# Convolutional attention block: how the first stage's normalisation steps are placed on the vector queue, where the first projections are accumulated, and which part of the values' tile is cleared

## Chip, core and metric

The kernel runs on one core of a Trainium2 chip as one launch. The metric is device time in microseconds (us), lower is better. The time before is the median of 3 runs.

## The reference, cut to what matters

The input is x, 8 images of 384 channels on a 32x32 grid, all float32. Four layers each add something to x. The change touches only the beginning of the first one:

```python
x = x + _L0(_gn(x), ...)          # _gn: 32 groups of 12 channels, mean and variance per image

def _dwproj(x, dw, g, b, pw):     # three times: for q, k and v
    y = conv3x3_depthwise(x, dw)
    y = gelu(_bn(y, g, b))        # _bn: mean and variance over all 8 images and the grid
    return einsum('oc,bchw->bohw', pw, y)

q, k, v = (_dwproj(x, ...).reshape(B, 8, 48, N) for each)
attn = softmax(einsum('bhcn,bhcm->bhnm', q, k) * scale)
out = _bn(einsum('oc,bchw->bohw', w_out, einsum('bhnm,bhcm->bhcn', attn, v)))
```

The batch norm over all images forces two passes. All depthwise convolutions have to be done, and their moments known, before the first gelu. The other layers (a mixture of experts, a ternary convolution, a deformable attention) are not touched.

## The kernel before

**First stage, about 0 to 230 us.** x is read from HBM as 16 tiles `xs`, normalised in place, convolved on TensorE, and written back raw to two scratch tensors in HBM, `rqk` and `rv`. The queues of all five engines are in an order written out by hand here (`manual_schedule`), so the order of the Python calls is the order of every queue.

The stage has eight *units* u = 0 to 7. A unit is two images (2k, 2k+1) and one half of the channels (h), that is two tiles xs (j = 0 and 1, one an image), each with two groups of rows (g). A unit's convolutions are cut into *pieces*, numbered n = 0 to 39 through the stage. Units 0 to 5 have five, `y0 a1 y1 a2 v0`; unit 6 has the first four; unit 7 has six, `y0 a1 y1 a2 v-1 v0`. "(u, i)" is piece i of unit u. A piece y is 48 matmul records, a piece a 96, a piece v 192 (L570[...]). For each piece, in this order on the queues:

1. some steps of the group normalisation of a later unit (below),
2. TensorE: the piece's matmuls into four banks of PSUM (`banks`), alternately four tiles of one bank each and two tiles `big` of two banks each. Two pieces can therefore be in PSUM at a time,
3. ScalarE: the copies of the four banks to a tile `y` in SBUF (L581, four copies of 512 columns or two of 1,024); `y` has four buffers,
4. VectorE: `bn_stats` of the four quarters of `y` (L587),
5. SyncE (SP): four DMAs of `y` to `rqk` or `rv` (L601). Up to two parts of a later tile xs (L292), or of image 0's raw maps (`g`, L225), are issued by SP ahead of the piece.

`norm(u)` makes the steps of a unit's normalisation. `begin(j)`: for both g, three `bn_stats` of xs (L351) and one `bn_aggr` (L354). `finish()`: a chain of small VectorE operations (L366 to L378), one power on GpSimd (L98), three more on VectorE (L380, L381, L385), of which the last writes `gss`, scale and shift. `apply(g, j)`: one ScalarE activation over 1,536 columns (L396) and two small products on GpSimd (L399). The table `steps` says which of a unit's seven steps is issued ahead of which piece:

```python
at = [(u - 2, 4) if u > 1 else (0, 0), (u - 1, 0), (u - 1, 0)]
at += [(u - 1, t) for t in range(1, 5)]
```

So `begin(0)` stands ahead of the last piece of unit u-2, `begin(1)` and the whole `finish` ahead of piece y0 of unit u-1, and the four `apply` ahead of that unit's next four pieces.

**End of the stage.** `spread_qk` and `spread_v` bring the moments of the maps together over partitions (matmuls `pmove` and `pmovev`) and `scale_of` makes scale and shift of the batch norm. `x_moments` has eight DMAs of SP (L508), ahead of the first piece of unit 7. `gelu_image` works on the raw maps of image 0. The first projections (L258) make q and k of the first pair of heads: for each of v = 0, 1 a tile `pq{v}_first` of two banks, of which `product` fills one half and then the other; each half is copied to `first_qk` (L620).

**Start of the attention stage, from 240 us.** `values_tile` makes the two tiles `vt` (128 partitions x 4,096), which hold the values as the second matmul of the attention wants them: blocks of 32 columns, of which 24 (`HQ0`) are values (L713, from `pv`), one is 1.0 (L688), and the rest zero. Each tile is cleared whole on GpSimd (L681) before. GpSimd is given the two clearings and then the two fills of ones. The attention's matmuls are `s` (L815) and `pav` (L830); `p` is the exponential on ScalarE (L822). From here on a scheduler orders all queues but ScalarE's.

Of the kernel before, what the change touches and what calls it, by code (L numbers as in the profile page):

```python
# [14 lines left out]
P = 128  # L15
KC = C // P
HALF = N // 2
# [12 lines left out]
HQ0 = HD0 // 2  # L30
# [25 lines left out]
def tile_kernel(ctx: ExitStack, tc: tile.TileContext, i: dict, out: bass.AP):  # L56
# [210 lines left out]
    with ExitStack() as pa:  # L267
# [71 lines left out]
        def norm(u):  # L339

            k, h = divmod(u, 2)
            mv = mvs[u % 2]
            turned = sa.tile([P, 2, 32], F32, tag="gp_t", name=f"gt{u}")
            rows = sa.tile([P, 2, 2, 16], F32, tag="gp_r", name=f"gr{u}")
            ss = sa.tile([P, 2, 32], F32, tag="gp_ss", name=f"gss{u}")
            small_ = sa.tile([P, 40], F32, tag="gp_s", name=f"gs{u}")

            def begin(j):
                for g in range(2):
                    for c in range(KC):  # L350
                        nc.vector.bn_stats(  # L351
                            xst[:, 2 * h + g, 2 * k + j, c, :], xs_of[2 * u + j][:, g * KC + c, :]
                        )
                    nc.vector.bn_aggr(  # L354
                        mv[:, :, 2 * j + g],
                        xst[:, 2 * h + g, 2 * k + j].rearrange("p c s -> p (c s)"),
                    )

            def finish():

                def owned(t):
                    return t.rearrange("p (g m d) -> p g m d", g=2, d=4)[:, :, :, 1:3]

                m8, v8, rs = small_[:, 0:2], small_[:, 2:4], small_[:, 4:6]
                dm, var, wide = small_[:, 8:40], turned[:, 1, :], [P, 2, 16]
                nc.vector.transpose(  # L366
                    turned.rearrange("p t y -> p (t y)"), mv.rearrange("p t y -> p (t y)")
                )
                nc.vector.tensor_reduce(m8, owned(turned[:, 0, :]), AX.XY, ALU.add)
                nc.vector.scalar_tensor_tensor(  # L370
                    dm.rearrange("p (g y) -> p g y", g=2), m8.unsqueeze(2).to_broadcast(wide),
                    -0.125, turned[:, 0, :].rearrange("p (g y) -> p g y", g=2),
                    ALU.mult, ALU.add,
                )
                nc.vector.tensor_tensor(dm, dm, dm, ALU.mult)
                nc.vector.tensor_tensor(dm, dm, var, ALU.add)
                nc.vector.tensor_reduce(v8, owned(dm), AX.XY, ALU.add)
                nc.vector.tensor_scalar(v8, v8, 0.125, 1e-5, ALU.mult, ALU.add)  # L378
                rsqrt(rs, v8, 2)
                nc.vector.tensor_copy(rows[:, 0], rs.unsqueeze(2).to_broadcast(wide))  # L380
                nc.vector.scalar_tensor_tensor(  # L381
                    rows[:, 1], m8.unsqueeze(2).to_broadcast(wide), -0.125, rows[:, 0],
                    ALU.mult, ALU.mult,
                )
                nc.vector.transpose(  # L385
                    ss.rearrange("p t y -> p (t y)"), rows.rearrange("p t g y -> p (t g y)")
                )

            def apply(g, j):
                n = 2 * j + g  # L390
                d = xs_of[2 * u + j][:, g * KC : g * KC + KC, :]
                sc, sh = ss[:, 0, n : n + 1], ss[:, 1, n : n + 1]
                if u == 0 and j == 1:
                    nc.vector.tensor_scalar(d, d, sc, sh, ALU.mult, ALU.add)
                else:
                    nc.scalar.activation(d, d, AF.Identity, bias=sh, scale=sc)  # L396
                for e, row in enumerate((0, HALF - W)):
                    f = d[:, :, row : row + W]
                    nc.gpsimd.tensor_tensor(  # L399
                        f, f, mrow[:, e : e + 1].unsqueeze(2).to_broadcast([P, KC, W]),  # L400
                        ALU.mult,
                    )

            return [lambda: begin(0), lambda: begin(1), finish] + [
                lambda g=g, j=j: apply(g, j) for g in range(2) for j in range(2)
            ]

        NU0 = 2 * NK
        work = []
# [3 lines left out]
        first = [[w[0] for w in work].index(u) for u in range(NU0)]  # L413
        steps = {}
        for u in range(1, NU0):
            at = [(u - 2, 4) if u > 1 else (0, 0), (u - 1, 0), (u - 1, 0)]
            at += [(u - 1, t) for t in range(1, 5)] if u < NU0 - 1 else [
                (u - 1, 1), (u - 1, 2), (u - 1, 3), (u, 0)
            ]
            for t, key in enumerate(at):  # L420
                steps.setdefault(key, []).append((u, t))

        def spread_qk():

            zs, nv, ng = (zy, zqk.rearrange("p c g s -> p (c g) s")), (3, 2), 16
            at = [slice(0, 96), slice(96, 160)]
            both = [
                room[:, 0, d].rearrange("p (v s g) -> p v s g", v=n, s=2)
                for d, n in zip(at, nv)
            ]  # L430
            v0 = 0
            for z, n, dst in zip(zs, nv, both):
                masked(z, n, v0, dst)
                v0 += n
            yield
            pm = bank("pmove")
            for t, d in enumerate(at):
                nc.tensor.matmul(
                    pm[:, d], lhsT=sels[:, t, :], rhs=room[:, 0, d], start=True, stop=True,
                )  # L440
            got = room[:, 1, :96].rearrange("p (x g) -> p x g", g=16)
            nc.vector.tensor_tensor(
                got, pm[:, :96].rearrange("p (x g) -> p x g", g=16),
                msk[:, :16].unsqueeze(1).to_broadcast([P, 6, 16]), ALU.mult,
            )
            fy = fs[:, :6].rearrange("p (v s) -> p v s", v=3)
            nc.vector.reduce_sum(fy.rearrange("p v s -> p (v s)"), got, AX.X)
            got = room[:, 1, 96:].rearrange("p (x g) -> p x g", g=8)
            nc.vector.tensor_tensor(
                got, pm[:, 96:160].rearrange("p (x g) -> p x g", g=8),  # L450
                msk[:, 16:24].unsqueeze(1).to_broadcast([P, 8, 8]), ALU.mult,
            )
            f = fs[:, 8:16]
            nc.vector.reduce_sum(f, got, AX.X)
            nc.vector.tensor_copy(
                fqk[:, :, :, 1:], f.rearrange("p (v s c) -> p v s c", v=2, s=2)
            )
            nc.vector.tensor_copy(fqk[:, :, :, 0], fy[:, :2])
            nc.vector.tensor_copy(fv[:, :, 0], fy[:, 2])
            for v in range(2):  # L460
                scale_of(v, fqk[:, v])
# [13 lines left out]
        def spread_v():  # L475

            both = sa.tile([P, 32], F32, tag="bothv", name="bothv")
            masked(zv, 2, 5, both.rearrange("p (c s g) -> p c s g", c=2, s=2))
            yield
            pm = bank("pmovev")  # L480
            nc.tensor.matmul(pm[:, :32], lhsT=sels[:, 1, :], rhs=both, start=True, stop=True)
            got = sa.tile([P, 4, 8], F32, tag="gotv", name="gotv")
            nc.vector.tensor_tensor(
                got, pm[:, :32].rearrange("p (x g) -> p x g", g=8),
                msk[:, 16:24].unsqueeze(1).to_broadcast([P, 4, 8]), ALU.mult,
            )
            f = sa.tile([P, 4], F32, tag="gotf", name="gotf")
            nc.vector.reduce_sum(f, got, AX.X)
            nc.vector.tensor_copy(
                fv[:, :, 1:].rearrange("p s c -> p c s"), f.rearrange("p (c s) -> p c s", s=2)  # L490
            )
# [26 lines left out]
        for n, (u, kind, s) in enumerate(work):  # L518
# [20 lines left out]
            if n == len(work) - 2:  # L539
                spread = spread_qk()  # L540
                next(spread)
            if n % 2:
                banks = [bank(f"pk{n}_{r}") for r in range(4)]
                outs = [(t, r, 1) for r, t in enumerate(banks)]
            else:
# [68 lines left out]
        next(ends)  # L614
        first_qk = image("first_qk")
        for v in range(2):
            pq = big(f"pq{v}_first")
            for h in range(2):
                product(pq[:, h * HALF : (h + 1) * HALF], 0, 0, v, h)
                (nc.vector.tensor_copy if v else nc.scalar.copy)(  # L620
                    first_qk[:, v, h * HALF : (h + 1) * HALF], pq[:, h * HALF : (h + 1) * HALF]
                )
            if v == 0:
                for _ in ends:
                    pass
                scales = scale_of(2, fv)
# [41 lines left out]
    with ExitStack() as pb:  # L668
# [9 lines left out]

        def values_tile(s):
            t = wb.tile([P, NT8, 2 * NH0, 32], F32, name=f"vt{s}")  # L680
            zero = nc.gpsimd.memset(t, 0.0)  # L681

            tc.add_manual_dep(
                zero.ins, scales.ins.name, mybir.DependencyInfo(
                    mybir.DependencyClass.Sync, mybir.DependencyReason.DATA
                ), reason="scales first",
            )
            nc.gpsimd.memset(t[:, :, :, HQ0 : HQ0 + 1], 1.0)  # L688
            vts.append(t)

        values_tile(0)
# [1476 lines left out]
```

## Time and profile before

| | us |
|---|---|
| time before, median of 3 (lowest, highest) | 3506.04 (3503.85, 3506.84) |
| the profiled execution's own time | 3505.04 |
| its span from the first to the last instruction | 3503.2 |
| TensorE busy over the span | 3380.1 (96%) |
| VectorE, ScalarE, GpSimd busy | 1697.7, 1297.4, 211.0 |
| pieces of the first stage: first matmul to the last copy to `y` | 24.56 to 230.90 |
| first matmul `pav` of the attention | 255.36 |

The profile is one execution on the chip. In the timeline a row begins with start and duration in us, then engine, line, operation, what is written and read, and how many instructions are merged in the row. In square brackets stands the idle time of the engine just before, and what ended it. PE is TensorE, DVE VectorE, ACT ScalarE, POOL GpSimd, SP SyncE; SPq is its queue, which issues DMAs. A table by windows gives each engine's busy time in each stretch, the granted share of TensorE's full clock (PEclk), the mean busy share of the 16 DMA engines, and what they moved.

### The profile page before, as it was taken

To read this page: it belongs to the slowest core of one execution; us is meant where nothing else is said; L and a number is where in the kernel's file an instruction comes from. 1 tells how busy PE (TensorE), PEld (TensorE's weight loads), DVE (VectorE), ACT (ScalarE), POOL (GpSimd) and SP (SyncE) were. 2 spreads that over 40 slices of the span, in tenths; PEclk is the share of its full clock that TensorE was granted. 3 is DMA by queue.
4 is the path that set the end of the run, shared out by engine and by line. 5 is a ranking of instruction groups with operands and counts; after the bars stand their busy time and mean duration, and the time that the engine had idled before them with its cause. 6 is when DMAs were issued, how large, how long until landed. Compare 5 with 4: busy or idle time off the path is not lost.

```text
span 3503.2 us, 44910 instructions
## 1 busy us (share of the span) xinstructions
PE 3380.1 (96%) x18599; PEld 1467.3 (42%) x18599; DVE 1697.7 (48%) x2881; ACT 1297.4 (37%) x1514; POOL 211.0 (6%) x231
## 2 busy tenths in 40 slices
PE   6889999999999999998999999999999999999888
PEld 3433434343434343443344445344453444534434
DVE  7862232323232323234266475663756637566573
ACT  4655444444444444433222322323223232232222
POOL 2110000000000000000000200102001020010112
PEclk9899999999999999999999999999999999999898
DMA  9972121212121212022600111101101011110000
GB/s 355 281 219 79 26 79 27 79 27 79 26 79 26 79 26 79 26 79 101 245 24 18 45 48 35 39 18 47 45 35 39 18 47 46 35 39 18 0 36 19
DMA packets 86259, 234.01 MB, mean 67 GB/s; under 512 B 21672, under 2 KB 21896, under 8 KB 79130
## 3 DMA queue, kind: packets, MB, share of 16 engines
q1 hardware_dynamic: 83882, 222.75, 19.9%
q10 hardware_dynamic: 1248, 4.72, 0.4%
q8 instruction: 150, 2.46, 0.3%
q0 software_dynamic: 912, 3.53, 0.3%
q14 instruction: 67, 0.55, 0.0%
HBM read 145.77 MB, written 75.59 MB: 63 GB/s over the span
## 4 chain that ended last, share of the span: by engine, by line
PE 42%; DVE 9%; ACT 1%; DMA 1%; issue 0%; POOL 0%; DVEq 0%; ACTq 0%; SPq 0%; POOLq 0%
PE y L1497 12%; PE ph L1476 9%; DVE y L1572 5%; PE pq L1617 4%; PE pw L1580 3%; PE pf L1924 3%; PE s L1795 2%; PE pav L1821 2%; DVE hd L1462 1%; PE pk L1770 1%; PE pv L1779 1%; PE pss L1834 1%; DMA o<-o 1%; PE xsb L1756 1%; PE plog L1226 1%; DVE off L1687 1%
## 5 line engine op out<-in xcount | busy, mean ns | idle before, releaser
L822 ACT ACTIVATE p<-s 128x1024 f32<-128x1024 f32 x512 | 496.3, 1021 | 368.7 <-PE s L815 368.5
L830 PE MATMUL pav<-p,vt 64*64 64x512 f32 x4096 | 494.7, 589 | 2.8 <-POOL vt L688 2.8
L1497 PE MATMUL y<-hd,w_sb 128*128 128x512 f32 x1080 | 488.7, 600 | 3.5 <-DVE hd L1462 3.5
L1476 PE MATMUL ph<-h,w_sb 128*128 128x512 f32 x1104 | 486.8, 595 | 3.1 <-ACT h L1425 3.0
L815 PE MATMUL s<-qk,qk 48*64 48x512 f32 x2944 | 355.1, 592 | 0.0
L1476 PEld LDWEIGHTS ph<-h,w_sb 128*128 128x128 f32 x1104 | 206.9, 190 | 264.4 <-issue 249.6
L1497 PEld LDWEIGHTS y<-hd,w_sb 128*128 128x128 f32 x1080 | 200.0, 191 | 248.2 <-issue 234.8
L830 PEld LDWEIGHTS pav<-p,vt 64*64 64x64 f32 x4096 | 168.0, 133 | 277.1 <-issue 273.2
L791 DVE COPY ta<-pav 128x512 f32<-128x512 f32 (+1 forms) x65 | 44.2, 682 | 475.5 <-PE pav L830 475.5
L1486 ACT ACTIVATE hd<-ph,b_sb 128x512 f32<-128x512 f32 x180 | 122.7, 682 | 312.7 <-PE ph L1476 312.7
L1572 DVE SCALAR_TENSOR_TENSOR y<-h,tap,y 128x961 f32<-128x961 f32 (+1 forms) x192 | 234.0, 1243 | 0.6
L570 PE MATMUL pk<-xs,cws_sb 32*32 32x496 f32 (+3 forms) x3840 | 175.4, 643 | 52.7 <-ACT y L581 26.0
L1687 DVE SCALAR_TENSOR_TENSOR off<-q,dw_sb,off 128x225 f32<-128x225 f32 (+3 forms) x432 | 212.0, 545 | 1.6
L815 PEld LDWEIGHTS s<-qk,qk 48*64 48x64 f32 x2944 | 109.3, 133 | 211.4 <-issue 190.5
L1812 ACT ACTIVATE p<-s 128x1024 f32<-128x1024 f32 x96 | 96.1, 1022 | 166.6 <-PE s L1795 141.7
L81 DVE COPY qk<-pq 128x512 f32<-128x512 f32 x46 | 31.8, 691 | 251.9 <-PE pq L258 251.9
L570 PEld LDWEIGHTS pk<-xs,cws_sb 32*32 32x32 f32 (+1 forms) x3840 | 87.2, 114 | 139.2 <-issue 53.5
L1462 DVE TENSOR_TENSOR hd<-hd,cb 128x512 f32<-128x512 f32 x180 | 122.4, 685 | 41.0 <-ACT hd L1486 40.8
L1580 PE MATMUL pw<-y,upw 128*128 128x512 f32 x288 | 130.4, 607 | 4.0 <-DVE y L1572 4.0
L1857 POOL TENSOR_TENSOR p<-p,p 128x1024 f32<-128x1024 f32 x48 | 112.9, 2354 | 349.9 <-ACT p L1812 349.8
L706 PE MATMUL pv<-wv_sb,g 128*128 128x384 f32 x384 | 127.2, 489 | 1.4 <-ACT g L243 1.4
L815 PE MATMUL s<-ql,ql 48*64 48x512 f32 x1024 | 128.2, 592 | 0.2 <-ACT p L822 0.2
(326 smaller groups left out, 3722.6 us busy)
## 6 DMA issues: line engine op xcount, KB each, us to landing
rqk<-y SPq DMA_DIRECT2D x96, 256.0 KB
g<-rqk SPq DMA_DIRECT2D x96, 256.0 KB
xs<-in_xs_dram SPq DMA_DIRECT2D x56, 384.0 KB
g<-rv SPq DMA_DIRECT2D x48, 256.0 KB
xh<-in_x_dram SPq DMA_DIRECT2D x48, 256.0 KB
f<-in_x_dram SPq DMA_DIRECT2D x24, 512.0 KB
f<-o SPq DMA_DIRECT2D x24, 512.0 KB
o<-ot SPq DMA_DIRECT2D x42, 256.0 KB
```

The costliest lines, as they stand in the source:

```text
L570: nc.tensor.matmul(banks[r][cols[q]].rearrange("p (h w) -> p h w", w=W)[:, :, c0:c1], lhsT=cws[rs, c, 2 * h + g, x, w], rhs=src[rs, :, c0 ...
L706: nc.tensor.matmul(pv[:, :C], lhsT=acts[b][2][:, c, t * P : (t + 1) * P], rhs=w_in[2][:, c, :], start=(c == 0), stop=(c == KC - 1),)
L815: nc.tensor.matmul(s[64 * k : 64 * k + 64, j * HALF : (j + 1) * HALF], lhsT=kt[r, k0 : k0 + 64], rhs=qt[r, h * HALF : (h + 1) * HALF], sta ...
L822: nc.scalar.activation(p, s, AF.Exp, scale=scale)
L830: nc.tensor.matmul(pav[k][64 * j : 64 * j + 64, :], lhsT=vts[b % 2][r, kc, 2 * hd : 2 * hd + 2, :].rearrange("p a b -> p (a b)"), rhs=p[r, ...
L1462: nc.vector.tensor_tensor(hd, hd, state["cb"], ALU.mult)
L1476: nc.tensor.matmul(ph, lhsT=w1[:, e, c, dc * P : (dc + 1) * P], rhs=state["h1"][c], start=(c == 0), stop=(c == KC - 1),)
L1497: nc.tensor.matmul(y, lhsT=w2[:, e, dc, m * P : (m + 1) * P], rhs=state[h, k], start=(k == 0), stop=(k == NE * KC - 1),)
L1572: nc.vector.scalar_tensor_tensor(d, f, tap2[:, c, t : t + 1], d, ALU.mult, ALU.add)
L1580: nc.tensor.matmul(pw[h], lhsT=upw2[:, c, m * P : (m + 1) * P], rhs=y[c][:, hs], start=(c == 0), stop=(c == KC - 1),)
L1617: nc.tensor.matmul(pq[h], lhsT=wq3[:, c, m * P : (m + 1) * P], rhs=h3[h][:, c, :], start=(c == 0), stop=(c == KC - 1),)
L1687: nc.vector.scalar_tensor_tensor(d, f, dw3[:, t : t + 1], d, ALU.mult, ALU.add)
```

## The change

The steps of `norm` become ten in place of seven: four `begin(j, g)` of one tile and one group each, `sums` (the former `finish` up to the power on GpSimd), `spread` (the three operations after it), and four `apply` in the same order as before. They are given places over two units, one ahead of most pieces:

| step of unit u | ahead of piece, before | ahead of piece, after |
|---|---|---|
| the four quarters of `begin` | (u-2,4) two, (u-1,0) two | (u-2,2), (u-2,3), (u-2,4), (u-1,0) |
| `sums` | (u-1,0) | (u-1,0) |
| `spread` | (u-1,0) | (u-1,1) |
| the four `apply` | (u-1,1) to (u-1,4) | (u-1,2), (u-1,3), (u-1,4), (u,0) |

For unit 1 what would come earlier than piece (0,0) is ahead of that piece; for unit 7 the last two `apply` are both ahead of (7,0), since unit 6 has no fifth piece.

Which pieces use the four single banks and which the two double ones is exchanged, and `pmove` and `pmovev` go to a double tile. Each of the four first projections gets a single bank of its own. Of `vt` only the columns 24 to 31 of each block are cleared, 1,024 elements in a partition in place of 4,096, and so the copies of the values (L713) no longer touch what GpSimd clears. No DMA is added, removed or moved: SP's queue has the same instructions in the same order. On GpSimd the order is the same too.

```diff
-            def begin(j):
-                for g in range(2):
-                    for c in range(KC):
-                        nc.vector.bn_stats(
-                            xst[:, 2 * h + g, 2 * k + j, c, :], xs_of[2 * u + j][:, g * KC + c, :]
-                        )
-                    nc.vector.bn_aggr(
...
-            def finish():
+            def begin(j, g):
+                for c in range(KC):
+                    nc.vector.bn_stats(
+                        xst[:, 2 * h + g, 2 * k + j, c, :], xs_of[2 * u + j][:, g * KC + c, :]
                     )
+                nc.vector.bn_aggr(
+                    mv[:, :, 2 * j + g],
+                    xst[:, 2 * h + g, 2 * k + j].rearrange("p c s -> p (c s)"),
+                )
...
+            def sums():
...
                 rsqrt(rs, v8, 2)
+
+            def spread():
+
                 nc.vector.tensor_copy(rows[:, 0], rs.unsqueeze(2).to_broadcast(wide))
...
-            return [lambda: begin(0), lambda: begin(1), finish] + [
-                lambda g=g, j=j: apply(g, j) for g in range(2) for j in range(2)
-            ]
+            pairs = [(a, b) for a in range(2) for b in range(2)]
+            return (
+                [lambda j=j, g=g: begin(j, g) for j, g in pairs] + [sums, spread]
+                + [lambda g=g, j=j: apply(g, j) for g, j in pairs]
+            )
...
-            at = [(u - 2, 4) if u > 1 else (0, 0), (u - 1, 0), (u - 1, 0)]
-            at += [(u - 1, t) for t in range(1, 5)] if u < NU0 - 1 else [
-                (u - 1, 1), (u - 1, 2), (u - 1, 3), (u, 0)
-            ]
-            for t, key in enumerate(at):
+            at = [(u - 2, 2), (u - 2, 3), (u - 2, 4), (u - 1, 0), (u - 1, 0), (u - 1, 1)]
+            at += [(u - 1, 2), (u - 1, 3), (u - 1, 4), (u, 0)]
+            for t, (u0, n) in enumerate(at):
+                key = (0, 0) if u0 < 0 else (7, 0) if (u0, n) == (6, 4) else (u0, n)
                 steps.setdefault(key, []).append((u, t))
...
-            pm = bank("pmove")
+            pm = big("pmove")
...
-            pm = bank("pmovev")
+            pm = big("pmovev")
...
-            if n % 2:
+            if n % 2 == 0:
                 banks = [bank(f"pk{n}_{r}") for r in range(4)]
...
         for v in range(2):
-            pq = big(f"pq{v}_first")
             for h in range(2):
-                product(pq[:, h * HALF : (h + 1) * HALF], 0, 0, v, h)
+                pq = bank(f"pq{v}_first{h}")
+                product(pq, 0, 0, v, h)
                 (nc.vector.tensor_copy if v else nc.scalar.copy)(
-                    first_qk[:, v, h * HALF : (h + 1) * HALF], pq[:, h * HALF : (h + 1) * HALF]
+                    first_qk[:, v, h * HALF : (h + 1) * HALF], pq
                 )
...
             t = wb.tile([P, NT8, 2 * NH0, 32], F32, name=f"vt{s}")
-            zero = nc.gpsimd.memset(t, 0.0)
+            tf = t.rearrange("p t h d -> p (t h) d")
+            zero = nc.gpsimd.memset(tf[:, :, HQ0:], 0.0)
...
-            nc.gpsimd.memset(t[:, :, :, HQ0 : HQ0 + 1], 1.0)
+            nc.gpsimd.memset(tf[:, :, HQ0 : HQ0 + 1], 1.0)
```

More of the change, by code (lines that the diff above doesn't have):

```diff
@@ L346, in norm @@
             small_ = sa.tile([P, 40], F32, tag="gp_s", name=f"gs{u}")
-            def begin(j):
-                for g in range(2):
-                    for c in range(KC):
-                        nc.vector.bn_stats(
-                            xst[:, 2 * h + g, 2 * k + j, c, :], xs_of[2 * u + j][:, g * KC + c, :]
-                        )
-                    nc.vector.bn_aggr(
-                        mv[:, :, 2 * j + g],
-                        xst[:, 2 * h + g, 2 * k + j].rearrange("p c s -> p (c s)"),
-                    )
-            def finish():
+            def begin(j, g):
+                for c in range(KC):
+                    nc.vector.bn_stats(
+                        xst[:, 2 * h + g, 2 * k + j, c, :], xs_of[2 * u + j][:, g * KC + c, :]
+                    )
+                nc.vector.bn_aggr(
+                    mv[:, :, 2 * j + g],
+                    xst[:, 2 * h + g, 2 * k + j].rearrange("p c s -> p (c s)"),
+                )
+            m8, v8, rs = small_[:, 0:2], small_[:, 2:4], small_[:, 4:6]
+            dm, var, wide = small_[:, 8:40], turned[:, 1, :], [P, 2, 16]
+            def sums():
                 def owned(t):
                     return t.rearrange("p (g m d) -> p g m d", g=2, d=4)[:, :, :, 1:3]
-                m8, v8, rs = small_[:, 0:2], small_[:, 2:4], small_[:, 4:6]
-                dm, var, wide = small_[:, 8:40], turned[:, 1, :], [P, 2, 16]
                 nc.vector.transpose(
```

## The prediction

> **What bounds the kernel now.** The page has TensorE busy for 96% of the span and idle visibly only in its first slices, so I read the first 256 us alone, first TensorE's timeline. Once a unit it stands still before a piece a2:
>
> ```profile
> 64.26 21.97 PE L570 MATMUL pk<-xs,cws_sb 32*32 32x512 f32 x480 [4.31 <-ACT y L581]
> 89.77 21.99 PE L570 MATMUL pk<-xs,cws_sb 32*32 32x512 f32 x480 [3.53 <-ACT y L581]
> 116.20 20.83 PE L570 MATMUL pk<-xs,cws_sb 32*32 32x512 f32 x480 [4.44 <-ACT y L581]
> ```
>
> All such gaps from 24.56 us to the end of the pieces sum to 28.1 us. Next, who holds ScalarE's copy back (timelines of VectorE and ScalarE, unit 2):
>
> ```profile
> 84.18 0.24 DVE L354 BATCH_NORM_AGGREGATE mvs<-xst 128x2 f32<-128x18 f32 x1
> ...
> 87.30 0.25 DVE L385 STREAM_TRANSPOSE gss<-gr 128x64 f32<-128x64 f32 x1
> 87.47 2.43 DVE L587 BATCH_NORM_STATS2 sy<-y 128x6 f32<-128x512 f32 x4
> 87.58 1.67 ACT L396 ACTIVATE xs<-xs,gss 128x1536 f32<-128x1536 f32 x1 [5.32 <-DVE gss L385]
> ```
>
> ScalarE waits 5.3 us for `gss`, and the copies of a1 are queued behind that `apply`; a2 needs their banks. Then the table by windows, whose last three columns are PEclk, DMA share, GB/s:
>
> ```profile
> 75.00:100.00 25.00, 21.41 (x471) 10.36 (x457) 21.80 (x47) 16.02 (x20) 2.95 (x8) 0.93 0.92 311
> 125.00:150.00 25.00, 20.58 (x454) 11.05 (x444) 20.93 (x46) 14.60 (x20) 3.29 (x9) 0.86 0.91 252
> ```
>
> VectorE (third figure) has 21 to 22 of 25 us, and the 16 DMA engines stand at 0.91 or more in every window from 25 to 200 us, whatever they move. So two others are close behind the wait. SP's timeline agrees:
>
> ```profile
> 85.45 2.14 SPq L292 DMA_DIRECT2D xs<-in_xs_dram  x2
> 87.69 0.99 SPq L601 DMA_DIRECT2D rqk<-y  x2
> ...
> 208.63 7.50 SPq L508 DMA_DIRECT2D xnst<-xst  x8
> 216.22 1.99 SPq L601 DMA_DIRECT2D rqk<-y  x2
> 222.24 1.93 ACT L581 COPY y<-pk 128x1024 f32<-128x1024 f32 x2 [6.34 <-DVE ss L496]
> ```
>
> Piece 10 was copied by 82.26 and is stored only from 87.69: SP is 5.4 us behind. The ScalarE row is piece 38. I read its wait as one for a `y` buffer, since piece 34's stores stand behind the `xnst` DMAs and the L496 named isn't its input. Last, the tail:
>
> ```profile
> 228.51 2.84 PE L258 MATMUL pq_first<-g,wq_sb 128*128 128x512 f32 x6
> 234.82 2.84 PE L258 MATMUL pq_first<-g,wq_sb 128*128 128x512 f32 x6 [3.47 <-ACT first_qk L620]
> 237.50 0.30 PE L481 MATMUL pmovev<-bothv,sels_sb 128*128 128x32 f32 x2
> ...
> 248.09 6.96 POOL L681 MEMSET vt<- 128x4096 f32 x2 [8.10 <-DVE xmv L144]
> 254.99 0.53 POOL L688 MEMSET vt<- 128x128 f32 x2
> 255.36 1.95 PE L830 MATMUL pav<-p,vt 64*64 64x512 f32 x16 [2.79 <-POOL vt L688]
> ```
>
> The second half of a projection waits for the copy of the first, and the first `pav` for GpSimd.
>
> [...]
>
> **Part 1, the norm steps.** Work on VectorE for a unit, start to start between 73.90 and 87.47 us: four quarters of `begin` 8.2, `sums` 1.5 (84.45 to 85.98), `spread` 0.6, and `bn_stats` of five pieces 5 x 2.43 = 12.2; together 22.5. The 26.0 us from 87.47 to 113.47 hold besides 0.9 of waiting for GpSimd's power and 2.6 for copies. Nothing is removed, but `spread` now has piece y0's 2.43 us ahead of it, which hide the power: 0.9 goes. Of the 2.6 I leave 0.6. The period becomes 23.1. `gss` of unit 1 comes later, not earlier: 35.3 + 2.4 - 0.8 = 36.9. Six periods on, unit 7's is ready at 36.9 + 6 x 23.1 = 175.5, before 191.5: 16 us.
>
> What is late next: after `gss` ScalarE has `apply` (1.6) and the copy of y1 (1.9), and only then has the v piece its banks; the first are free 2.6 us after `gss`. A2 needs the banks of a1 alone, which is copied ahead of that `apply`, so it no longer waits. TensorE now stands 2.5 to 3.7 us before v, and v may start at half clock[...]. Its copy then ends 2.6 + 10.3 + 1.9 = 14.8 us after `gss`. VectorE comes to v's moments after three `bn_stats` of y and three quarters of `begin`, 3 x 2.4 + 3 x 2.05 = 13.4, and waits about a half us for the first half of the copy; that is the 0.6. The last `apply` is behind the v copy: 1.9 + 1.6 + 1.0 (GpSimd's masks, as 61.65 to 64.26) make 4.5 us after v, when y0 (2.78) and three quarters of a1's first pass (0.8) are done. A new wait of 0.9 us, off VectorE's path. On GpSimd the power of `sums` is queued behind those masks, which end 2 us sooner.
>
> **The stores then set the end.** SP's issues and order are unchanged, and while it is never idle it can't go faster. Idle gaps of SP in its timeline: 3.3 at 35.6 (piece 1 is now copied 4 us sooner, being ahead of the first `apply`, but piece 2 only at 36.9 + 1.6 + 1.9 = 40.4, before 42.3: 1.9 gained), then 1.7 at 63.4, 0.9 at 116.1, 0.2, 2.8 at 127.6, 3.0 at 139.9, 0.5, 1.8 at 167.7, 0.3: 13.1 us. All can go, since copies lead by then. Piece 34's stores, and with them the copy of piece 38, come 13.1 us sooner: 209.1. VectorE's 16 us are more, so the smaller counts. After it ScalarE has, as before, table, three gelus and the copy of piece 39: it ends at 230.9 - 13.1 = 217.8 = e.
>
> **Part 2, projections.** Before, e to the gelu of v (240.61) took 9.7 us. Now both halves run without the copy; `pmovev` follows VectorE's moments at e + 3.2, its chain takes 2.7 to 2.9 (237.84 to 240.57), the gelu starts at e + 6.2: 3.5 us. The swap of banks changes a copy by 0.1 us and costs nothing, in ScalarE's slack (15 of 25 us).
>
> **Part 3, the clearing.** GpSimd's 7.3 us in front of the ones become 2 x 1,024/4,096 x 3.5 + 0.3 = 2.1 if the price is by element. Bounds: by the ones (128 elements, stride 32, 0.27 us) 1,024 would take 2.1 each, 4.5 in all; still under the 7.3. The wait of 2.79 goes; TensorE's own work is next. From the gelu: pq1 ends after 2.8, `pv` 2.2, `s` 2.0, `pv` 2.1, `s` 1.9: `pav` at 11.0, before 14.75; 3.8 us. After it TensorE is at 99%, so what is gained stays.
>
> **Sum.** 13.1 + 3.5 + 3.8 = 20.4. Against the profiled execution's 3505.04 (its span and 1.8 around it) 3484.6; the median of the runs stands 1.0 above that execution: **3485.6 us**.
>
> **Rivals.**
> - *Stores bound* (above), 0.54: 3485.6, own range 3479 to 3493.
> - *DMA isn't a limit*, 0.19: SP's issues take 0.32 us when quick and about 0.9 in the mean, so they may speed up when spread evenly. Then VectorE sets the end: from unit 7's `gss` on, `apply`, copy, `apply`, copy, two `apply` take 10.2 us, the last masks are done at 11.3, the rest of a1 takes 2.5, y1 2.8, a2 3.4, the two v 6.9 each, the copy 1.9: 35.7, so piece 39 is copied by 211.2, 19.7 sooner; with 7.3 it is 27: 3479. At the most the whole 28.1 goes: 3470.
> - *The stall only moves*, 0.20: v wholly at half clock (13.7) makes VectorE's period 16.3 + 1.9 + 1.2 + 2.1 + 1.5 + 2.4 + 0.6 = 26.0, as before. Then only the tail's 7.3 and some 2 of the start: 3497. That the strided clearing gains nothing falls here.
> - *Slower*, 0.07: stores slow down when they crowd. The windows from 25 to 225 us have a mean of 294 GB/s, 58.7 MB. If it falls under 274 (125 to 150 us had 252), the stage takes 14.3 us more, which overturns the tail: 3506.04 + 14.3 - 7.3 = 3513. Against it: the same packets, and the lowest rates stand where SP paused.
>
> **How the numbers follow.** About 0.2%, 7 us, can be told from no change. Faster: 0.54 + 0.19 + 0.13 of the third = 0.86; same: the rest of the third, 0.07; slower 0.07. Range 3474 to 3499: it leaves out the third's upper half, the slower case and the extreme of the second.
>
> **What would show it.** In the profile after: `gss` starts some 23 us apart; TensorE's gaps before v, not a2; SP without gaps from 45 to 200 us; piece 38 copied near 209; `pq_first` with no wait for L620; L686's clearings 0.9 to 2 us each. I am wrong if SP still pauses and piece 38 still comes near 222, or if the GB/s fall as the gaps close.

## The result and the profile after

The kernel after the change takes 3492.06 us (median of six runs, 3487.57 to 3494.72); the kernel before, run beside it, 3506.9. The ratio is 0.9958 with a 95% interval of 0.9945 to 0.997, so the change brings 10.5 to 19.3 us, 14.7 by the ratio. The forecast was 20 us, at 3485.6 with a range of 3474 to 3499. The profiled execution took 3494.72 (span 3492.9), the slowest of the six, so I compare places in its trace, not its total.

TensorE's timeline, the same stretch as before:

```profile
67.87 29.57 PE L574 MATMUL pk<-xs,cws_sb 32*32 32x496 f32 x656 [1.94 <-issue]
98.63 22.25 PE L574 MATMUL pk<-xs,cws_sb 32*32 32x512 f32 x480 [1.19 <-POOL xs L402]
121.80 16.76 PE L574 MATMUL pk<-xs,cws_sb 32*32 32x512 f32 x391 [0.92 <-POOL xs L402]
```

The waits of 3.5 to 4.4 us before a2 are gone. What is left in this stretch is 0.9 to 1.9 us: the first gap lies inside piece 9, a v piece, the other two inside a piece a1 that waits for GpSimd's masks, as the prediction expected. The norm chain of unit 3, from the last `bn_aggr` to the `apply` (timelines of VectorE, ScalarE and GpSimd):

```profile
77.04 0.24 DVE L353 BATCH_NORM_AGGREGATE mvs<-xst 128x2 f32<-128x18 f32 x1
...
78.75 2.46 DVE L591 BATCH_NORM_STATS2 sy<-y 128x6 f32<-128x512 f32 x4
...
78.99 0.70 POOL L98 TENSOR_TENSOR gs<-gs,mhalf 128x2 f32<-128x2 f32 x1 [3.06 <-DVE gs L378]
81.14 0.16 DVE L383 COPY gr<-gs 128x32 f32<-128x32 f32 x1
...
81.56 0.24 DVE L388 STREAM_TRANSPOSE gss<-gr 128x64 f32<-128x64 f32 x1
81.73 2.43 DVE L591 BATCH_NORM_STATS2 sqk<-y 128x6 f32<-128x512 f32 x4
81.84 1.67 ACT L399 ACTIVATE xs<-xs,gss 128x1536 f32<-128x1536 f32 x1 [0.93 <-DVE gss L388]
```

Piece y0's moments run while GpSimd makes the power, and ScalarE waits 0.9 us for `gss`, where it waited 5.3. The transposes that write `gss` start at 36.7, 58.7, 81.6, 104.3, 127.4, 150.5 and 176.1 us for units 1 to 7. Now the stretch from 50 to 200 us in one window, first the kernel before, then after (time, then busy time of TensorE, its weight loads, VectorE, ScalarE and GpSimd; last PEclk, DMA share, GB/s):

```profile
50.00:200.00 150.00, 124.89 (x2693) 62.67 (x2693) 127.46 (x275) 92.48 (x109) 18.49 (x50) 0.89 0.92 290
```

```profile
50.00:200.00 150.00, 137.57 (x2886) 57.48 (x2884) 131.28 (x291) 101.66 (x120) 20.48 (x56) 0.99 0.92 299
```

TensorE is busy for 12.7 us more and hardly ever loses its clock: of these 150 us the granted clock was 0.50 for 34.1 us in the kernel before, in six stretches of 3.4 or 6.8 us, and now for 3.4 us in one. But the DMA share stays at 0.92, and the rate rises by only 9 GB/s. Where the stage ends, ScalarE now names its wait (timelines of SP and ScalarE):

```profile
204.60 6.96 SPq L512 DMA_DIRECT2D xnst<-xst  x8
211.66 1.04 SPq L605 DMA_DIRECT2D rqk<-y  x2
...
217.02 2.05 ACT L585 COPY y<-pk 128x512 f32<-128x512 f32 x4 [7.30 <-DMA rv<-y]
```

Piece 38 is copied at 217.02 (before 222.24), after 7.3 us of waiting for the stores that free a buffer `y`. Piece 39's copy ends at 225.70 (before 230.90). This is not only so at the end. ScalarE's longest waits from 30 to 232 us, first before, then after (what is waited for, us in total, times, the longest):

```profile
ACT xs L396 <- DVE gss L385: 39.6, 7, 6.7
```

```profile
ACT y L585 <- DMA rv<-y: 24.7, 12, 7.3
ACT y L585 <- DMA rqk<-y: 18.1, 8, 4.2
```

Before, ScalarE waited for `gss`; now it waits 42.8 us for stores to land. The tail (timelines of TensorE and GpSimd):

```profile
221.68 5.96 PE L258 MATMUL pq_first<-g,wq_sb 128*128 128x512 f32 x12
228.58 0.38 PE L485 MATMUL pmovev<-bothv,sels_sb 128*128 128x32 f32 x2 [0.94 <-DVE bothv L474]
...
236.89 1.84 POOL L686 MEMSET vt<- 128x1024 f32 x2 [5.75 <-DMA gbias_sb<-in_gbias_dram]
238.67 0.55 POOL L693 MEMSET vt<- 128x128 f32 x2
...
241.94 1.90 PE L835 MATMUL pav<-p,vt 64*64 64x512 f32 x16
```

All twelve matmuls of a projection run without the wait for L620's copy (now L624), the clearings take 0.92 us each, and the first `pav` comes at 241.94 without waiting for GpSimd, 13.4 us sooner than before. From the last copy to `pav` it takes 16.24 us, where it took 24.46.

### The profile page after: what moved, and what is told of

Its sections match the earlier page's. It is cut to its first block, busy times and chain, and to the rows that moved or that the text cites. A ratio compares the mean times of both kernels' runs of the same rounds, so it can differ in the third digit from the quotient of the medians.

```text
span 3492.9 us, 44919 instructions
## 1 busy us (share of the span) xinstructions
PE 3384.1 (97%) x18599; PEld 1458.3 (42%) x18599; DVE 1696.7 (49%) x2881; ACT 1298.5 (37%) x1514; POOL 206.1 (6%) x231
## 4 chain that ended last, share of the span: by engine, by line
PE 41%; DVE 9%; DMA 1%; ACT 1%; POOL 0%; issue 0%; DVEq 0%; ACTq 0%; POOLq 0%; SPq 0%
PE y L1502 12%; PE ph L1481 10%; DVE y L1577 5%; PE pq L1622 4%; PE pw L1585 3%; PE pf L1929 3%; PE s L1800 2%; PE pav L1826 2%; DVE hd L1467 1%; DMA o<-o 1%; PE pk L1775 1%; PE pv L1784 1%; PE xsb L1761 1%; PE pss L1839 1%; PE plog L1231 1%; DVE off L1692 1%
## 5 line engine op out<-in xcount | busy, mean ns | idle before, releaser
L574 PEld LDWEIGHTS pk<-xs,cws_sb 32*32 32x32 f32 (+1 forms) x3840 | 77.7, 111 | 139.4 <-issue 54.0
L1929 PE MATMUL pf<-att,wp_sb 128*128 128x512 f32 x288 | 127.6, 598 | 0.5 <-DVE x L1937 0.5
```

Source lines behind the costliest of these rows:

```text
L574: nc.tensor.matmul(banks[r][cols[q]].rearrange("p (h w) -> p h w", w=W)[:, :, c0:c1], lhsT=cws[rs, c, 2 * h + g, x, w], rhs=src[rs, :, c0 ...
L1929: nc.tensor.matmul(pf[:, hs], lhsT=wp3[:, pr, m * P : (m + 1) * P], rhs=att[:, pr, hs], start=(pr == 0), stop=(pr == NPAIR3 - 1),)
```

## The experiments

My theory after the result: VectorE's period shortened as worked out, but the 16 DMA engines pace the stage behind it, so the stage gives back only what they can move faster. The tail adds its own saving, independently of that. Rivals: SP's issuing paces the stores; VectorE still sets the end; the projections and the clearing bring everything. Each ratio below is to the kernel before, run beside that experiment; each trace is one execution.

### One part at a time

`norm_only` keeps the spread steps and takes the rest back:

```diff
-            if n % 2 == 0:
+            if n % 2:
...
+            pq = big(f"pq{v}_first")
...
-            zero = nc.gpsimd.memset(tf[:, :, HQ0:], 0.0)
+            zero = nc.gpsimd.memset(t, 0.0)
```

> The new places of the norm steps alone; banks, first projections and the clearing of vt as before. Theory (the DMA engines pace the first stage, so that of the 13 us forecast for it only the 5.2 us seen in the profile after can be had): last copy to y near 225.7 us, then the old tail of 24.5 us to the first pav, at about 250; some 5 us off the time of before, 3501 to 3503 us. Rival (the new steps themselves are worth their 13 us and the exchanged banks cost 8 of them): last copy near 218, 13 us off, 3494. Second rival (the steps gain only with the exchanged banks): last copy at 229 to 231, the time of before.

Measured: 3500.05 us, ratio 0.9983 (0.9976 to 0.9989), so 3.9 to 8.4 us. The last copy is at 226.29, as in the full change. TensorE's timeline shows both waits of the tail again:

```profile
230.21 4.43 PE L258 MATMUL pq_first<-g,wq_sb 128*128 128x512 f32 x6 [4.66 <-ACT first_qk L624]
...
252.34 1.95 PE L834 MATMUL pav<-p,vt 64*64 64x512 f32 x16 [2.79 <-POOL vt L692]
```

In this execution the waiting half of the projection took 4.43 us, where it took 2.84 before, so `pav` comes only 3.0 us sooner than before.

`tail_only` is the other half: the steps as before, the banks exchanged, own banks for the projections, the gaps alone cleared.

```diff
-            pq = big(f"pq{v}_first")
...
+                pq = bank(f"pq{v}_first{h}")
+                product(pq, 0, 0, v, h)
...
-            zero = nc.gpsimd.memset(t, 0.0)
+            zero = nc.gpsimd.memset(tf[:, :, HQ0:], 0.0)
```

> The kernel before with the projections in banks of their own, the exchanged banks and the clearing of the gaps; the norm steps as before. Theory (the parts add up, and the tail from the last copy to the first pav fell from 24.5 to 16.2 us by itself): last copy near 230.9, first pav near 247.2, 8 us off the time of before, 3498 to 3500 us. Rival (the tail could only shrink because the stage's end was held up by the stores, so that TensorE was done early): tail of 20 us or more, 4 us off.

Measured: 3494.76 us, ratio 0.997 (0.9959 to 0.9981), so 6.7 to 14.4 us. The gain is larger than I expected (3498 to 3500 us). The last copy is at 231.27, where it was, and `pav` at 247.52: 16.25 us from one to the other, as in the full change. The two parts add up within their intervals (6.0 and 10.5 by the ratios, together 14.7), and each acts at its own place.

`gaps_only` is the kernel before with only the clearing changed:

```diff
-            zero = nc.gpsimd.memset(t, 0.0)
+            tf = t.rearrange("p t h d -> p (t h) d")
+            zero = nc.gpsimd.memset(tf[:, :, HQ0:], 0.0)
```

> The kernel before with only the values' tile cleared in its gaps. Expected: the last copy stays at 230.9 us, the first projections still wait 4.6 us for banks, and the pav, which waited for GpSimd's clearing at the end, comes 2.8 to 3.8 us sooner (first pav 251.6 to 252.6, before 255.4); time 3502.7 to 3503.7 against 3506.5. Rival, that the clearing was hidden behind the wait for banks and only both together pay: first pav within 0.5 us of 255.4 and time unchanged.

Measured: 3505.63 us against 3509.97, ratio 0.9989 (0.9981 to 0.9998). TensorE's timeline:

```profile
237.60 5.48 PE L258 MATMUL pq_first<-g,wq_sb 128*128 128x512 f32 x6 [4.66 <-ACT first_qk L620]
242.88 0.34 PE L481 MATMUL pmovev<-bothv,sels_sb 128*128 128x32 f32 x2
...
257.81 1.90 PE L831 MATMUL pav<-p,vt 64*64 64x512 f32 x16
```

In this execution the stage ended 2.8 us later and the waiting projection ran slower (5.48 us for six matmuls, 2.84 before). So `pav` comes later than before instead of the 2.8 to 3.8 us sooner that I expected, and from the last copy to `pav` it takes 24.14 us, hardly less than 24.46. From `pmovev` to `pav`, where the clearing acts, it takes 14.93 us in place of 17.86. That is 2.9 us, about the 2.79 that `pav` had waited for GpSimd, and `pav` no longer names GpSimd. By the ratio the clearing alone brings 0.7 to 6.7 us, so it pays without the own banks.

The runs so far also show how far single traces differ. With the old norm steps the last copy ends at 230.90, 231.27 and 233.67 us (before, `tail_only`, `gaps_only`), with the new ones at 225.70, 225.33 and 226.29 (the kernel after, twice, and `norm_only`). The gain of the steps is clear of that spread; a difference of 2 or 3 us between two traces is not.

### Fewer bytes, more bytes

`fewer_loads` doesn't read six of the sixteen x tiles (9.4 MB); the earlier tile that the edit names is used in their place.

```diff
+        AGAIN = {8: 4, 9: 5, 10: 6, 13: 5, 14: 6, 15: 7}
...
+                    if m in AGAIN:
+                        xs_of[m] = xs_of[AGAIN[m]]
+                    else:
+                        loads += load_tile(m, 4 * (nc.sync,))
```

> The kernel after, but six of the sixteen tiles xs (8, 9, 10, 13, 14, 15) are not read from HBM: the units take an earlier tile that lies in SBUF already (the values computed are then not the reference's). 24 DMAs of 384 KB, 9.4 MB of the stage's 72, are left out; every instruction of the engines stays. Theory (the DMA engines pace the stage after the change): the stores come sooner, VectorE sets the end, gss stays 22 to 23 us apart to the last unit, the last copy to y at 210 to 215 in place of 225.7 and the time 10 to 15 us under the kernel after, about 3479. Rival (ScalarE's copies or VectorE hold the end, and the waits named DMA are only the last of several): last copy within 3 us of 225.7, the time as after.

Measured: 3474.66 us, ratio 0.991 (0.9895 to 0.9925). The last copy comes at 209.35, 16.4 us sooner than in the kernel after and a little sooner than expected. The table by windows:

```profile
50.00:200.00 150.00, 140.32 (x3210) 63.03 (x3209) 140.31 (x331) 104.94 (x126) 20.42 (x56) 0.99 0.87 255
```

The DMA share falls to 0.87 and VectorE rises to 140 of 150 us. `gss` has a period of 22.1 us from unit to unit, where the kernel after goes from 22.0 up to 25.6. With fewer bytes VectorE is the bound through most of the stage; ScalarE's waits for stores fall from 42.8 to 10.0 us, of which 6.1 stand before piece 38. This run takes 24 transfers off SP as well, so it can't tell the engines from SP's issuing. The opposite run says more: `more_loads` copies the same 9.4 MB a second time into memory that nobody reads, issued by GpSimd, and SP keeps what it has.

```diff
+                if m in AGAIN:
+                    nc.gpsimd.dma_start(
+                        out=again[AGAIN.index(m), d],
+                        in_=src[2 * k + j, 1 - d % 2, :, h * w : (h + 1) * w],
+                    )
```

> The changed kernel, which besides loading the x tiles 8, 9, 10, 13, 14 and 15 copies the same 9.4 MB once more, into memory nobody reads, issued by GpSimd: SP's queue keeps its transfers, the 16 DMA engines get 9.4 MB more. Theory, the DMA engines pace the stage and SP is held up behind them: 9.4 MB at the 314 GB/s of 25 to 200 us are 30 us, less the 7% of 175 us (12 us) in which the engines are idle: last copy to y 18 to 30 us later than 225.7 us, time 3510 to 3522 us. Rival, SP's issuing paces the stores and the engines have room: last copy within 4 us, time 3492 to 3496. Rival, VectorE paces: time unchanged.

Measured: 3506.31 us, ratio 0.9995 (0.9987 to 1.0003), so all that the change had brought is lost. The table by windows, and ScalarE's copies of pieces 38 and 39:

```profile
50.00:200.00 150.00, 130.19 (x2698) 52.80 (x2696) 124.03 (x268) 92.22 (x110) 27.64 (x68) 0.95 0.95 330
```

```profile
233.13 2.05 ACT L592 COPY y<-pk 128x512 f32<-128x512 f32 x4 [7.69 <-DMA rv<-y]
...
239.91 1.89 ACT L592 COPY y<-pk 128x1024 f32<-128x1024 f32 x2
```

The last copy ends 16.1 us later than in the kernel after, although SP has the same transfers in the same order and now waits for 32.9 us from 45 to 200 us (5.8 in the kernel after). By the trace's packet records the 16 engines were fully busy (1.00) while SP paused. TensorE's waits for GpSimd's masks are as before (6.5 us, 6.4 in the kernel after), so it isn't GpSimd's issuing that delays the pieces. In this run, then, the engines and not SP hold the stores back. I had expected 18 to 30 us, and it was less. As a rough account: with a second issuer the engines moved 330 GB/s in place of 299, and 31 GB/s over 150 us are 4.7 MB, half of what was added; the other 4.7 MB at 299 GB/s are 15.7 us. The added copies go from HBM to HBM; what such a copy costs beside a load into SBUF is not shown.

### Another issuer for the same bytes

`pool_loads` has GpSimd issue the x tiles 8 to 12, with no byte more or less.

```diff
-                    loads += load_tile(m, 4 * (nc.sync,))
+                    loads += load_tile(m, 4 * (nc.gpsimd if m < 13 else nc.sync,))
```

> The changed kernel with the x tiles 8 to 12 (5 of 16) issued by GpSimd in place of SP. Theory, DMA engines: bytes and order of need are the same, SP gets gaps of 5 x 4 x 0.5 to 0.9 = 10 to 18 us, but the stores wait as long for the engines; last copy at 224 to 228 us, time within 3 us of after_again (3489 to 3495). Rival, SP's issuing paces the stores: its 10 to 18 us fewer of issuing let the last copy come at 212 to 218 us, time 3480 to 3486. A third case: GpSimd, waiting for a tile to be free, holds up its own copies and masks, TensorE's pieces wait for them, and the time rises by 5 us or more; then pieces show waits for POOL over 2 us.

`after_again` is the kernel after, run beside it:

> The changed kernel once more, beside the others on the same chip. 3490 to 3494 us, last copy to y near 225.7 us, first pav near 242, half clock in two stretches only.

Measured: 3485.73 us for `pool_loads` (0.9936, 0.9922 to 0.9949), 3492.73 for `after_again` (0.9956, 0.9943 to 0.997). The intervals overlap a little; the traces differ where they should: last copy at 220.64 against 225.33. That is neither of my two cases, 224 to 228 or 212 to 218, and the time lies in the rival's range (3480 to 3486). SP's waits from 45 to 200 us, first in the kernel after, then in `pool_loads` (what is waited for, us in total, times, the longest):

```profile
SPq L605 <- ACT y L585: 3.3, 5, 1.6
SPq L605 <- ACT xs L399: 1.3, 3, 0.5
SPq L605 <- DMA rqk<-y: 0.6, 1, 0.6
SPq L292 <- POOL gs L98: 0.6, 1, 0.6
```

```profile
SPq L605 <- DMA rqk<-y: 14.2, 10, 2.1
SPq L605 <- ACT y L585: 12.3, 10, 3.5
SPq L605 <- ACT xs L399: 3.3, 6, 0.8
SPq L605 <- DMA rv<-y: 1.6, 4, 0.7
SPq L512 <- DVE sy L591: 1.3, 1, 1.3
```

SP's waits grow by 27 us and the last copy gains 4.7, so what SP saves in issuing is not what arrives at the end. The table by windows has the same DMA share as the kernel after and a somewhat higher rate:

```profile
50.00:200.00 150.00, 135.47 (x2982) 55.93 (x2987) 133.18 (x298) 103.31 (x124) 27.84 (x70) 0.99 0.92 305
```

6 GB/s over 150 us are 0.9 MB, worth 3.0 us at 299 GB/s: most of the 4.7. In the packet records the tiles 8 to 12 differ: their packets of 12,288 bytes took 506 ns in the mean with GpSimd as the issuer and 617 with SP in the kernel after. The tiles 13 to 15, which SP issues in both, took 630 and 627. No run here separates the issuer from the loads being earlier (the last packets of tile 12 start at 91 us in place of 102) or from SP's saved issuing, so the reason for the gain stays open.

### The last stores

`xm_late` issues the eight small transfers of `x_moments` ahead of piece 38 instead of piece 34:

```diff
-            if u == NU0 - 1 and at == 0:
+            if n == len(work) - 2:
                 x_moments()
```

> The kernel after, but the eight DMAs of x_moments are issued by SP ahead of piece 38 in place of piece 34, behind the stores of pieces 34 to 37. Theory (the y buffers wait for the stores, and SP's 7 us for these DMAs stand in front of piece 34's): piece 38 is copied near 210 to 212 us in place of 217, but piece 37 still waits for piece 33's stores, and pmove, the moments and the first gelu hang on piece 37; so the last copy to y comes at 222 to 224 in place of 225.7, 2 to 3 us off the time of after. Rival (SP's time is the limit, not what is behind which): last copy 7 us sooner. Second rival: VectorE's xmv then waits for these DMAs and the tail grows by 3 us or more.

Measured: 3489.43 us, 0.9953 (0.9939 to 0.9967), not separable from the kernel after by its time. Piece 38 is copied at 210.45, after 1.28 us of waiting for a store in place of 7.3. But the last copy ends only at 223.26 (225.70), because other things are then late: in the trace the gelu ahead of it waits 2.4 us for its scale and the copy itself 1.6 more. As expected, this hangs on piece 37, copied at 207.24 (207.79).

`late_v` moves image 0's raw v maps (six transfers) there too, ahead of `x_moments`:

```diff
-                    for v, t in acts[0].items():
-                        loads += fetch_raw(t, v, rqk[0], rv[:, 0])
+                    for v in (1, 0):
+                        loads += fetch_raw(acts[0][v], v, rqk[0], rv[:, 0])
...
+            if n == len(work) - 2:
+                for f in fetch_raw(acts[0][2], 2, rqk[0], rv[:, 0]):
+                    f()
```

> xm_late and with it the v maps of the first feature (the six transfers of g2 that stood ahead of piece 33) are issued ahead of piece 38, x_moments after them. Theory that the 16 DMA engines pace the end of the stage: 1.5 MB that nobody needs before v make way for 26 stores, the last copy to y falls from 223.3 to about 218.5 us, the first pav from 239.9 to about 235.5, time about 3485 us, unless the v maps now come too late for the first projections of v, which would show as a wait for DMA on g or its copy after 226 us and take back up to 4 us (3489). Rival, SP's issues and not the bytes pace the stores: the same number of issues stands ahead of the last stores but for six, 6 x 0.9 = 5.4 us less, so this run alone does not tell them apart; pool_loads does. Rival, VectorE paces the stage: last copy stays at 223, time 3489.

Measured: 3494.24 us, 0.9962 (0.9948 to 0.9975). The last copy came at 219.54, near what I expected, but the time is above both of my values: `pav` is at 242.13, as late as in the kernel after. The timelines of SP and ScalarE:

```profile
219.48 6.82 SPq L512 DMA_DIRECT2D xnst<-xst  x8
226.39 7.27 SPq L607 DMA_DIRECT2D rv<-y  x8
...
236.86 1.28 ACT L829 ACT_TABLE_LOAD   x1 [7.50 <-DMA gbo_sb<-in_gbo_dram]
```

The exponential waits 7.5 us for a DMA. It doesn't read the constant `gbo_sb` that is named. The stores of the last two v pieces, now behind fourteen other transfers, left SP's queue at 233.66, a little before. I take it that `p` reuses memory of the first stage and waits for them to land. In `xm_late` these stores leave SP's queue at 232.48, and the exponential, from 235.74, names its matmul `s` instead. No run puts the reading to the test, so it stays argued.

`pool_xm` and `pool_late` combine: GpSimd issues the five tiles and also `x_moments` in the first; GpSimd issues the five tiles and SP `x_moments` late in the second.

```diff
                 for e in range(2):
-                    nc.sync.dma_start(
+                    nc.gpsimd.dma_start(
                         out=xnst.rearrange("p b c e s -> p (b c) e s")[32 * g : 32 * g + 32, :, e],
```

> pool_loads and in addition the eight small transfers of x_moments issued by GpSimd, at the same place in the program, so that SP goes from piece 33's stores straight to piece 34's. In pool_loads SP spent 6.9 us issuing them (199.8 to 206.7) and piece 38's copy waited for a free y buffer until 212.0 us. If SP's time is what holds the last stores: last copy to y 4 to 6 us sooner than pool_loads (220.6), 215 to 217 us, time 3480 to 3482 us. If it is the engines' time for the 7700 packets of 24 bytes, which stay: last copy within 2 us of 220.6, time 3484 to 3487. If GpSimd's issuing of so many packets is slow and its next power (ss at L98, 217 us in after) waits, pq_first waits for g and the time is 3488 or more.

```diff
-                    loads += load_tile(m, 4 * (nc.sync,))
+                    loads += load_tile(m, 4 * (nc.gpsimd if m < 13 else nc.sync,))
...
-            if u == NU0 - 1 and at == 0:
+            if n == len(work) - 2:
                 x_moments()
```

> pool_loads and xm_late together: x tiles 8 to 12 loaded by GpSimd, x_moments issued by SP ahead of piece 38. xm_late alone took the last copy from 225.7 to 223.3 us and the time by 3 us; pool_loads alone to 220.6 and by 7 us. If both act on the same thing, the queue of stores ahead of piece 38, and VectorE's period of 22.1 us then bounds the stage, the sum is less than both: last copy 217 to 219.5 us, time 3482 to 3485 us. If piece 39's stores, now behind x_moments, hold up what reuses y's memory (the weights p of the first attention unit), the wait before p is 2 us or more and the time is 3486 to 3490.

Measured: `pool_xm` 3483.46 us, 0.9928 (0.9914 to 0.9941); `pool_late` 3481.91 us, 0.993 (0.9916 to 0.9943). By the ratios these two and `pool_loads` (0.9936) can't be told apart, so no gain from placing `x_moments` otherwise is shown on top of the loads. The times of `pool_xm` and `pool_late` do lie below the kernel after, with intervals that end where its interval begins.

In `pool_xm` SP comes to piece 34's stores at 202.6, where `pool_loads` has 206.8, and piece 38 is copied at 209.28 (211.96). Yet the last copy is at 222.41, not sooner than in `pool_loads`. That is inside the case "within 2 us", which laid it to small packets that stay. But they don't stay: with SP as the issuer the trace has 6,144 of 24 bytes (not 7700), with GpSimd 128 of 1,152 bytes for the same transfers. A nearer reason is that piece 37, on which the end hangs, was copied at 206.04 (203.70).

In `pool_late` the last copy is at 214.48 and `pav` at 230.99, further than I expected. But unit 7's `gss` comes at 171.6 there and at 174.9 in `pool_loads`, and up to that point the two programs are the same. Half of the difference is therefore one between executions. What holds in all three is that with the loads on GpSimd this `gss` comes at 171.6 to 174.9 us, and with SP as the only issuer at 175.4 to 176.6 (the kernel after, twice, `norm_only`, `xm_late`, `late_v`). The table by windows of `pool_late`:

```profile
50.00:200.00 150.00, 139.68 (x3170) 59.97 (x3168) 135.91 (x306) 104.63 (x126) 27.85 (x70) 0.99 0.94 316
```

## Why the prediction was right, and which term was not

**The likeliest case came true.** The stores bound the stage after the change: ScalarE's waits name them, and `more_loads` and `fewer_loads` move the end with the bytes. The measured time is inside that case's own range (3479 to 3493), near its upper end.

**Norm steps: right.** `gss` was forecast at 36.9 us for unit 1 and 175.5 for unit 7, with a period of 23.1. It came at 36.7 and 176.1; the first periods are 22.0 to 23.1, the last 25.6 (22.5 in `pool_loads`). The 10.3 us that the forecast carried for a v piece starting at half clock were an estimate, and mostly they didn't come: PEclk is 0.99 from 50 to 200 us, and v took 7.4 to 9.4 us in the pieces 9, 14, 19, 24 and 29. TensorE doesn't stand ahead of v for 2.5 to 3.7 us; what gaps there are lie mostly inside it and are under 2 us.

**"All can go", SP's idle gaps of 13.1 us: the mis-sized term.** It measured 4.6 us at piece 34's stores (216.22 to 211.66) and 5.2 at the last copy (230.90 to 225.70). Most gaps did go, as forecast. SP's waits for `y` from 45 to 200 us were in the kernel before

```profile
SPq L601 <- ACT y L581: 12.2, 10, 2.9
```

and are 3.3 now. But the forecast let each issue keep its length, and they grew. Between the first store and piece 34's stores SP has the same 194 transfers in all kernels with its queue unchanged. Its pauses in between fell from 20.3 to 9.5 us, 10.8 us less, and its issues took 160.5 us in place of 155.1, which takes back half of it (0.83 us in the mean in place of 0.80; the forecast had about 0.9). The other runs agree: 156 to 157 us with the old steps (`tail_only`, `gaps_only`), 160 to 161 with the new (`after_again`, `norm_only`). What lengthens an issue is not shown; in `more_loads`, with the engines busier, the same 194 took 151.3.

The packet records show why little was to be had. In the pauses that SP made before from 45 to 200 us, the engines were busy for 0.93 of the time, as in the whole stretch (0.92): they were working off what was queued. The sentence "while it is never idle it can't go faster" was an assumption, and the 151.3 to 161 us of issuing for the same 194 transfers don't bear it out; that each of SP's pauses was lost time was wrong. Seen from the bytes, the change made the engines carry 9 GB/s more over 150 us, 1.3 MB, which at 299 GB/s is 4.5 us. The share stood in the profile, and I used it only to name the bound, not to size it.

**Projections and clearing: 7.3 forecast, 8.2 in the trace** (24.46 to 16.24 from the last copy to `pav`). The clearing by element at 2.1 us for two was near: 1.84. `gaps_only` puts 2.9 us on the clearing alone, so the rest, 5.3, would go to the banks; that is a subtraction, no run has the banks alone. The forecast had divided it 3.5 and 3.8, which makes too little of the banks and too much of the clearing.

**The sum.** 20.4 forecast; the traces give 5.2 + 8.2 = 13.4, and the runs 14.7 by the ratio (10.5 to 19.3). By the ratios of the parts the norm steps brought 6.0 where 13.1 was forecast, and the rest 10.5 where 7.3 was. That the sum came as near as it did is therefore in part luck: one term was over twice too large, the other too small.

**The rivals.** "DMA isn't a limit" falls by `more_loads` and by ScalarE's 42.8 us of waiting for stores. "The stall only moves" falls by the period of `gss`. "Slower" falls by the rate, which rose instead of falling under 274 GB/s. The forecast counted on nothing from another issuer, yet the last copy came 4.7 us sooner in the trace of `pool_loads` (220.64 against 225.33), with the loads ahead of the stores given to GpSimd.

## What to carry to other kernels

When the next bound is a transfer queue, look at what the DMA engines do in the pauses of the issuing engine before you count these pauses as a gain: here the engines were busy for 0.93 of them, and of 13.1 us 5.2 were gained. Spread long steps of the engine that feeds the others singly between short ones: here the stall of 3.4 to 4.4 us a unit went, and PEclk rose from 0.89 to 0.99. When the end is paced by stores, try another issuer for the loads ahead of them: the kernels that did so ran some 7 to 10 us faster than the kernel after here by the ratios (`pool_loads`, `pool_xm`, `pool_late`).

## What the runs showed of the hardware that I had not expected

- The same load packets were quicker from a second issuer: 501 to 514 ns in the mean for tiles 8 to 12 issued by GpSimd (`pool_loads`, `pool_xm`, `pool_late`), 584 to 629 when SP issued them among its stores (the kernel after, twice, `norm_only`, `xm_late`, `late_v`). Why is open. The gain in rate is less sure: 301, 305 and 316 GB/s from 50 to 200 us against 298 to 300, at shares of 0.92 to 0.94 in both groups. With the added copies it was 330 at 0.95.
- The time for which SP was busy issuing the same transfers was not fixed. A store took 0.31 us to issue when quickest, and in the mean 0.77 in the kernel before and 0.82 in the kernel after; an unchanged queue of 194 transfers took SP from 151 us (`more_loads`) to 161 us of issuing.
- Eight small transfers of 18 KB each went out as 6,144 packets of 24 bytes with SP as the issuer and as 128 of 1,152 bytes with GpSimd (`pool_loads`, `pool_xm`).
- Clearing a tile in blocks of 8 elements out of 32 cost GpSimd nearly by the element: 1.84 us for two of 1,024 (the kernel after), where two of the whole 4,096 took 6.96 (the kernel before).
